# Bi-directional WKV and mixture-of-experts kernel on one core: one scan run over the other, shared outputs added in a second array, and a new order around layer 0's end

## The chip, the core and the metric

The kernel runs as one program on one core of a Trainium2 chip. Its time is the device time of one execution in microseconds (us); the figure for a kernel is the median of its timed runs, and lower is better. A core has the engines TensorE (PE), VectorE (DVE), ScalarE (ACT), GpSimd (POOL) and SyncE (SP), each with a queue of its own that runs in order, and 16 DMA engines that the queues feed.

## What is computed

x is [4, 512, 512]: 4 batches of 512 tokens of 512 channels, 2048 tokens in all. Two layers follow each other, x = x + ffn_l(cond_l(x, k)), with the same k (named fside) for both. The condition is a WKV in both directions of the sequence. For a batch and a channel:

```python
tf    = sigmoid(sum(time_emb))                       # one number of a batch
decay = exp(-exp(w)) * (0.5 + 0.5 * tf)
ek, ekv = exp(minimum(k, 30)), exp(minimum(k, 30)) * k
# forward:  a_t = a_{t-1} * decay + ekv_t,  b_t = b_{t-1} * decay + ek_t   -> nf, df
# backward: the same from the last token to the first                     -> nb, db
euk = exp(minimum(u + k, 30))
num = nf + nb - ekv + euk * k
den = df + db - ek + euk
out = sigmoid(x) * (num / maximum(den, 1e-8)) * (0.8 + 0.2 * tf)
```

Layer 0's ffn is an RMS norm, a router that sends each token to 2 of 8 experts (hidden width 256) and one shared expert of width 256 for all tokens. Layer 1's has 32 experts of hidden width 352, 6 for a token with a capacity of 512 tokens each, and a wider shared expert.

## The kernel before

Tokens are taken in 16 tiles of 128 (tile t belongs to batch t // 4). `acc` holds x in SBUF as rows of tokens, `kA` holds k turned to channels by tokens, `zT` the condition's output in the same form, both in 16 columns of 128 channels by 512 tokens. Two arrays in HBM, `xa` and `xb`, collect layer 0's output by rows; the routed experts add their rows to the one and the other in turn.

**Scan loop.** It runs over 16 units n (batch b = n // 4, channel chunk c = n % 4), one unit further in each stage: `turn(n + 3)` turns k's rows `kr` to `kA` (PE, then an ACT copy) and, after a batch's last chunk, issues the load of the next batch's `kr`, of which there is one buffer; `front` (L406, L408) and `front_exps` (L414) make ek and euk; `mid` multiplies by k (L425, L426) and calls `scans`, which runs four scans of 512 steps on DVE, forward (L263) and reversed (L264), for ek and for ekv. `sums` (L431) adds forward, reversed and own term on PE in PSUM, three products for den and three for num, and ACT makes r = 1 / den by Relu, Ln and Exp (L440 to L442). `back` (L449 to L452) corrects r once and multiplies num, r and the sigmoid of x into `zT`. The constants of w, u and tf are built ahead of the loop (L211 to L221).

**What else stands in the loop.** A batch later, its condition is turned back to rows (`row_turn`, `row_out`) and written to HBM (`z0d`), the router's logits follow, and routing in small DVE steps: `route_v` (the norm's scale, L501), `route_max`, `route_top` (r0sm, L291), `route_pos`, `route_pay`, `route_slots`, and POOL writes the slot tables by indirect DMA (L353). The shared expert runs for tiles 0 to 5 at units 7, 10 and 13 (`pairs0`): `share_up` (PE), `share_silu` (ACT), `share_hid` (DVE), `share_turn` and `share_down` (PE), `share_add` (L612, DVE, on top of `acc`, written to xa). `exps1_upto` makes layer 1's ek and euk on ACT (L627, L628) into columns that are free. Ahead of the loop, POOL zeroes the tables and all of xb in 16 writes (L254), and the last three tiles of x are copied to xa (L571).

**Tail.** After the loop come batch 3's rows (pz) and routing and the shared tiles 6 to 12.

**Routed layer 0.** `routed(0, ...)` goes through the slots of 128 tokens. Each gathers rows of z (POOL, L768), turns them (`turn_rows`, PE pza L781, scaling to zgT on ACT L785), multiplies by gate and up (L833, L837), forms the hidden rows on POOL (hrow, L844), turns them (phT, L795), multiplies by down (pout, L809) and adds rows to xa or xb (L814, POOL). Each turning is done one slot later, so a last `turn_hidden`, `copy_hidden` and `put_out` stand behind the loop over experts; branches on the experts' counts (L891) stand between. Beside it DVE works through `wkv1` (L907), layer 1's WKV: four scans, two adds of forward and reversed (L915, L916), a reciprocal (L921).

**Late tiles and second condition.** Behind the last turning the shared expert runs for tiles 13 to 15 (from `LATE`). Then the z1 stage (L960 to L985) goes through the 16 tiles: load xa and xb, add, turn (pt), sigmoid on ACT, product with `kA` on DVE (L975), logits (plg, L977), turn to rows (pz, L982), copy (zr) and write. The logits lg (L990) and layer 1's shared expert (L1058) follow.

**Order.** In the scan loop and the tail the orders of ACT, PE and DVE are those of the code; in routed layer 0 those of POOL, PE and ACT (`manual_schedule`). All other orders (SP throughout, POOL in the loop, DVE in routed layer 0, everything in the z1 stage) are chosen by the scheduler.

Of the kernel before, what the change touches and what calls it, by code (L numbers as in the profile page):

```python
# [25 lines left out]
DEN_MIN = 1e-8  # L26
EXP_LN = "natural_log_exp_and_others"
# [3 lines left out]
def adaln_ffn_kernel(  # L31
# [90 lines left out]
    def load_k(b):  # L122
        kr = wk.tile([P, TB, D], F32, tag="kr", name=f"kr{b}", bufs=1)
        nc.sync.dma_start(kr, kf[b * S : (b + 1) * S, :].rearrange("(i p) c -> p i c", p=P))
        return kr
# [54 lines left out]
    kr = wk.tile([P, TB, D], F32, tag="kr", name="kr0", bufs=1)  # L180
    for i in range(TB):
        nc.scalar.dma_start(kr[:, i, :], kf[i * P : (i + 1) * P, :])
    load_x(0)
    gaten = acc[:E1, NT - 3, :]
# [9 lines left out]
            engines={mybir.EngineType.Activation, mybir.EngineType.PE, mybir.EngineType.DVE}  # L194
# [20 lines left out]
    for l in range(2):  # L215
# [8 lines left out]
        decay.append(dec)  # L224
# [20 lines left out]
    for tb, width in ((table0, 3), (table1, 2)):  # L245
        blank = wk.tile([P, NCOL * width], F32, name=f"blank{width}", tag="lgT", bufs=1)
        bv = blank.rearrange("p (c w) -> p c w", w=width)
        nc.gpsimd.memset(bv, 0.0)
        nc.gpsimd.memset(bv[:, :, 0], EMPTY)
        nc.gpsimd.dma_start(tb.rearrange("(p c) w -> p (c w)", p=P), blank)  # L250
    zero = wk.tile([P, D], F32, name="zero", tag="zr", bufs=TB)
    nc.gpsimd.memset(zero, 0.0)
    for t in range(NT):
        nc.gpsimd.dma_start(xb[t * P : (t + 1) * P, :], zero)  # L254


    L = S - 1

    def scans(l, b, c, ek, ekv, df, dx, nf, nx):

        dec = decay[l][:, c, b : b + 1]
        for v, f, r in ((ek, df, dx), (ekv, nf, nx)):
            nc.vector.tensor_tensor_scan(f, dec.to_broadcast([P, S]), v, 0.0, ALU.mult, ALU.add)  # L263
            nc.vector.tensor_tensor_scan(  # L264
                r[:, L - 1 :: -1],
                v[:, L:0:-1],
                dec.to_broadcast([P, L]),
                0.0,
                ALU.add,
                ALU.mult,  # L270
            )

# [113 lines left out]
    def turn(n):  # L386

        nonlocal kr
# [4 lines left out]
        for i in range(TB):  # L393
            nc.tensor.transpose(pk[:, i * P : (i + 1) * P], kr[:, i, c * P : (c + 1) * P], ident)
        nc.scalar.copy(kA[:, c, b * S : (b + 1) * S], pk)
        if c == NC - 1 and b + 1 < NB:
            kr = load_k(b + 1)
            load_x(b + 1)

    def front(n):  # L400
# [4 lines left out]
        ek = wk.tile([P, S], F32, tag="ek", name=f"ek{n}", bufs=2)  # L405
# [706 lines left out]
```

## Time and profile before

| what | value |
|---|---|
| median of 3 runs | 1581.71 us (1581.02 to 1586.45) |
| the profiled execution | 1576.35 us, with a span of 1574.6 |
| mean granted clock of TensorE | 0.969 |
| PE busy | 1441.3 us (92%), weight loads beside it 858.7 |
| DVE busy | 681.8 us (43%) |
| POOL busy | 582.0 us (37%) |
| ACT busy | 407.1 us (26%) |
| DMA | 184.97 MB, 117 GB/s over the span |

All lines further on come from one profiled execution. Its own time is 1576.35 us; the span, from the first instruction to the last, is 1.75 shorter. Times in the text count from the span's start. In the rows of 40 slices a slice is 39.4 us, and a digit is the busy share in tenths; PEclk is the clock that TensorE was granted, in tenths of full speed. A row of the groups names line, engine, operation and tile, then the busy time, the mean of one instruction, and the idle time ahead of it with what ended it. PE was busy for 92% of the span, but at different clocks: in the stretch from 550 to 600 us it was granted 0.69 on average.

### The profile page before, as it was taken

What the parts mean: (1) busy time and instruction counts of PE and PEld (TensorE: products, weight loads), DVE (VectorE), ACT (ScalarE), POOL (GpSimd) and SP (SyncE); (2) the same over time, 40 slices, a digit from 0 to 9 for tenths busy, and PEclk for the clock granted to TensorE, in tenths of its full rate; (3) what the DMA queues carried; (4) which work ended last, traced back from release to release, by engine and by line L of the source; (5) the groups of instructions that cost most, each with busy time, mean ns of one, the idle gap of its engine ahead of it and who ended that gap; (6) DMA issues with size and microseconds to landing.
All of it is one profiled execution on the core that took longest, in us unless ns stands there. A gap on an engine that the chain in (4) does not pass through costs nothing. (4 is left out here: it accounts for less than half of the span.)

```text
span 1574.6 us, 16451 instructions
## 1 busy us (share of the span) xinstructions
PE 1441.3 (92%) x5097; PEld 858.7 (55%) x5097; DVE 681.8 (43%) x1192; ACT 407.1 (26%) x969; POOL 582.0 (37%) x576
## 2 busy tenths in 40 slices
PE   4978988989778698999999999999999999999997
PEld 2444555757556484444444565555655555555554
DVE  6897965999990045341111222222222222222221
ACT  4755634464344232000000111111111111111110
POOL 3010234666555100046662333344334344343332
PEclk8999989999999969999999999999999999999999
DMA  9201114454545652001115464666645495555442
GB/s 350 88 28 41 41 41 167 84 114 69 134 96 133 179 179 92 0 1 56 34 66 163 119 175 100 172 175 163 171 93 156 107 289 107 153 163 145 113 104 36
DMA packets 117179, 184.97 MB, mean 117 GB/s; under 512 B 19928, under 2 KB 65004, under 8 KB 117016
## 3 DMA queue, kind: packets, MB, share of 16 engines
q1 hardware_dynamic: 80120, 122.14, 22.8%
q0 software_dynamic: 36336, 60.04, 20.3%
q8 instruction: 66, 1.08, 0.3%
q10 hardware_dynamic: 576, 1.05, 0.2%
q14 instruction: 81, 0.66, 0.1%
HBM read 152.07 MB, written 52.64 MB: 130 GB/s over the span
## 5 line engine op out<-in xcount | busy, mean ns | idle before, releaser
L809 PE MATMUL pout<-w,hT 128*128 128x512 f32 (+1 forms) x432 | 202.8, 602 | 3.7 <-ACT hT L800 2.9
L833 PE MATMUL pgate<-w,zgT 128*128 128x352 f32 (+1 forms) x656 | 193.2, 438 | 10.9 <-PEq L891 6.7
L837 PE MATMUL pup<-w,zgT 128*128 128x352 f32 (+1 forms) x656 | 189.6, 432 | 0.0
L814 POOL DMA_INDIRECT out_dram<-ob,put x52 | 83.0, 1596 | 281.1 <-DVE ob L813 137.4
L768 POOL DMA_INDIRECT acc<-z1d,put x119 | 123.6, 1038 | 134.7 <-PE pza L781 59.9
L353 POOL DMA_INDIRECT table<-pay,r1sloti x96 | 93.6, 975 | 199.3 <-DVE hid L1061 172.4
L849 DVE SCALAR_TENSOR_TENSOR hrow<-pup,tab,sgt 128x352 f32<-128x352 f32 x84 | 49.1, 584 | 254.1 <-issue 131.2
L833 PEld LDWEIGHTS pgate<-w,zgT 128*128 128x128 f32 x656 | 122.8, 195 | 66.0 <-issue 17.5
L837 PEld LDWEIGHTS pup<-w,zgT 128*128 128x128 f32 x656 | 123.0, 191 | 49.0
L813 DVE COPY ob<-pout 128x512 f32<-128x512 f32 x84 | 58.1, 692 | 174.7 <-PE pout L809 167.3
L809 PEld LDWEIGHTS pout<-w,hT 128*128 128x128 f32 (+1 forms) x432 | 77.5, 194 | 71.3 <-issue 54.7
L353 POOL DMA_INDIRECT table<-r0pay,r0sloti x32 | 36.1, 1128 | 182.8 <-DVE r0sloti L343 137.8
L781 PEld LDWEIGHTS pza<-ident,acc 128*128 128x128 f32 x584 | 72.7, 142 | 53.8 <-issue 27.7
L781 PE MATMUL pza<-ident,acc 128*128 128x128 f32 x584 | 88.2, 276 | 12.9 <-DMA acc<-z0d,put 9.8
L804 ACT COPY hT<-phT 96x128 f32<-96x128 f32 x84 | 22.1, 263 | 287.4 <-DVE hT L802 282.8
L768 POOL DMA_INDIRECT acc<-z0d,put x51 | 69.7, 1367 | 71.9 <-PE pgate L833 27.2
L1058 PE MATMUL g<-zT,w 128*128 128x512 f32 (+1 forms) x192 | 88.6, 605 | 4.4 <-DVE lg L990 4.4
L791 ACT COPY zgT<-pza 128x256 f32<-128x256 f32 x103 | 38.4, 373 | 209.1 <-DVE zgT L790 153.4
L809 PE MATMUL pout<-zT,hT 128*128 128x512 f32 (+1 forms) x192 | 87.8, 592 | 0.0
L795 PE MATMUL phT<-ident,hrow 128*96 128x128 f32 (+1 forms) x322 | 55.9, 276 | 33.3 <-DVEq L891 15.0
L1058 PE MATMUL u<-zT,w 128*128 128x512 f32 (+1 forms) x192 | 86.3, 592 | 0.0
L1067 PE MATMUL o<-w,hid 128*128 128x512 f32 (+1 forms) x192 | 83.8, 592 | 0.0
(277 smaller groups left out, 2158.4 us busy)
## 6 DMA issues: line engine op xcount, KB each, us to landing
w<-in_L_ffn_w_dram SPq DMA_DIRECT2D x44, 704.0 KB
zT<-in_L_ffn_w_dram SPq DMA_DIRECT2D x20, 704.0 KB
w<-in_L_ffn_w_dram SPq DMA_DIRECT2D x22, 512.0 KB
zT<-in_L_ffn_w_dram SPq DMA_DIRECT2D x10, 512.0 KB
w<-in_L_ffn_w_dram SPq DMA_DIRECT2D x22, 192.0 KB
xb<-zero POOLq DMA_DIRECT2D x16, 256.0 KB
acc<-in_x_dram SPq DMA_DIRECT2D x4, 1024.0 KB
z0d<-zr SPq DMA_DIRECT2D x16, 256.0 KB
```

Of the source, the lines that this page charges most:

```text
L353: ins = nc.gpsimd.indirect_dma_start(out=table, out_offset=bass.IndirectOffsetOnAxis(ap=sloti[:, t, j : j + 1], axis=0), in_=pay[:, t, j, ...
L768: nc.gpsimd.indirect_dma_start(out=rows(e, s), out_offset=None, in_=zd, in_offset=bass.IndirectOffsetOnAxis(ap=put_at[:, e * NS + s : e * ...
L781: nc.tensor.transpose(pza[which][:, c * P : (c + 1) * P], rows(e, s)[:, c * P : (c + 1) * P], ident)
L795: nc.tensor.transpose(phT[:m, j * P : (j + 1) * P], hrow[:, f : f + m], ident)
L809: nc.tensor.matmul(po, hT[:m, j, :], dv[:m, j, :], start=(j == 0), stop=(j == nf - 1))
L813: nc.vector.tensor_copy(row, po)
L814: nc.gpsimd.indirect_dma_start(out=outs[n % len(outs)], out_offset=bass.IndirectOffsetOnAxis(ap=at, axis=0), in_=row, in_offset=None, boun ...
L833: nc.tensor.matmul(pg, zt[:, c, :], gv[:, c, :], start=(c == 0), stop=(c == NC - 1))
L837: nc.tensor.matmul(pu, zt[:, c, :], uv[:, c, :], start=(c == 0), stop=(c == NC - 1))
L849: nc.vector.scalar_tensor_tensor(hrow, pu, tab[:, col, 1:2], sgt, ALU.mult, ALU.mult)
L1058: nc.tensor.matmul(p[:m], wv[:, c, f : f + m], zT[:, c, cols], start=(c == 0), stop=(c == NC - 1))
L1067: nc.tensor.matmul(po, hid[:m, j, i * P : (i + 1) * P], dv[:m, j, :], start=(j == 0), stop=(j == len(FCH) - 1))
```

## The change

- **Scans.** The decay is held below 1 (`NEAR_1`). With om = 1 - decay^2, a reversed scan of v whose first column is then multiplied by 1 / om, followed by a forward scan of the result, gives (forward + reversed - own) / om. So the exponent of ek gets a bias of ln(om), and the sum comes out of one array. The scans work in place on `v`, which holds ek and ekv side by side; `sums` has two products for each output instead of three, and `wkv1` drops both adds.
- **k's rows.** `kr` has two buffers; batch 1's load is issued before the loop, and that of batch b + 2 at the end of batch b.
- **Shared outputs.** `share_put` takes the place of `share_add`: ACT copies the product to SBUF and SP writes it to xb's rows, instead of a DVE add to x. x itself is written to xa by SP, a batch at a time, and only xb's three late tiles are zeroed.
- **Routing.** The steps stand one to four units later: `route_v` at the next unit ahead of `front_exps`, `route_top` and `route_pay` at c = 3, `route_pos` and `route_slots` at the next batch's c = 0, with the slot writes spread over three units. The writes of all batches are now in the group that doesn't wait for each other. `share_hid` stands behind `back`. POOL's order is that of the code, too.
- **Routed layer 0.** DVE's order, `wkv1` included, is that of the code. The last turning is returned as `finish()`, and tile 13's share_up, share_silu and share_hid stand ahead of it. The late tiles' outputs go to columns of `zT`.
- **z1 stage.** SP's order is that of the code: xa and xb of the three late tiles first, then blocks of four tiles (1 MB), block 0's xb into a free column of zT, the others into buffers of their own. The order of the tiles' work is unchanged.

```diff
-        kr = wk.tile([P, TB, D], F32, tag="kr", name=f"kr{b}", bufs=1)
+        kr = wk.tile([P, TB, D], F32, tag="kr", name=f"kr{b}")
...
     load_x(0)
+    krs.append(load_k(1))
...
-        decay.append(dec)
+        nc.vector.tensor_scalar(dec, dec, NEAR_1, None, ALU.min)
+        om = const.tile([P, NC, B], F32, name=f"om{l}")
+        nc.vector.tensor_scalar(om, dec, -1.0, 1.0, ALU.mult, ALU.add)
+        nc.vector.scalar_tensor_tensor(om, dec, 1.0, om, ALU.add, ALU.mult)
+        lom = const.tile([P, NC, B], F32, name=f"lom{l}")
+        nc.scalar.activation(lom, om, AF.Ln)
+        inv = const.tile([P, NC, B], F32, name=f"inv{l}")
+        nc.vector.reciprocal(inv, om)
+        cap = const.tile([P, NC, B], F32, name=f"cap{l}")
+        nc.vector.tensor_scalar(cap, om, E30, None, ALU.mult)
+        decay.append((dec, cap, lom, inv))
...
+    def blank_tables():
...
-    for t in range(NT):
-        nc.gpsimd.dma_start(xb[t * P : (t + 1) * P, :], zero)
...
-    def scans(l, b, c, ek, ekv, df, dx, nf, nx):
-
-        dec = decay[l][:, c, b : b + 1]
-        for v, f, r in ((ek, df, dx), (ekv, nf, nx)):
-            nc.vector.tensor_tensor_scan(f, dec.to_broadcast([P, S]), v, 0.0, ALU.mult, ALU.add)
...
+    def scans(l, b, c, v):
+
+        dec, _, _, inv = (m[:, c, b : b + 1] for m in decay[l])
+        for h in range(2):
             nc.vector.tensor_tensor_scan(
...
+                v[:, h, ::-1], dec.to_broadcast([P, S]), v[:, h, ::-1], 0.0, ALU.mult, ALU.add
             )
+        nc.vector.tensor_scalar(v[:, :, 0], v[:, :, 0], inv, None, ALU.mult)
+        for h in range(2):
+            nc.vector.tensor_tensor_scan(v[:, h, :], dec.to_broadcast([P, S]), v[:, h, :], 0.0, ALU.mult, ALU.add)
...
-            kr = load_k(b + 1)
             load_x(b + 1)
+            if b + 2 < NB:
+                krs.append(load_k(b + 2))
...
+            nc.scalar.activation(v[:, 0, :], v[:, 0, :], AF.Exp, bias=decay[0][2][:, c, b : b + 1])
+            nc.scalar.activation(euk, euk, AF.Exp)
...
-            nc.tensor.matmul(p, m, f, start=True, stop=False)
-            nc.tensor.matmul(p[:, :L], m, r[:, :L], start=False, stop=False)
...
+            nc.tensor.matmul(p, m, d, start=True, stop=False)
             nc.tensor.matmul(p, m, o, start=False, stop=True)
...
-        zr = wk.tile([P, D], F32, tag="zr", name=f"zr{t}", bufs=TB)
+        zr = wk.tile([P, D], F32, tag="zr", name=f"zr{t}", bufs=3)
...
-    nc.sync.dma_start(xa[LATE * P :, :], xf[LATE * P :, :])
...
-    def share_add(t):
-        nc.vector.tensor_tensor(acc[:, t, :], shared_up.pop(t), acc[:, t, :], ALU.add)
-        nc.sync.dma_start(xa[t * P : (t + 1) * P, :], acc[:, t, :])
+    def share_put(t):
+
+        so = wk.tile([P, D], F32, tag="so", name=f"so_rows{t}")
+        nc.scalar.copy(so, shared_up.pop(t))
+        nc.sync.dma_start(xb[t * P : (t + 1) * P, :], so)
...
+        if n == 1:
+            for t in range(LATE, NT):
+                nc.gpsimd.dma_start(xb[t * P : (t + 1) * P, :], zero)
+        if n == 2:
+            blank_tables()
+        if c == 2 and b < NB:
+            nc.sync.dma_start(
+                xa[b * S : (b + 1) * S, :].rearrange("(i p) c -> p i c", p=P), acc[:, b * TB : (b + 1) * TB, :]
+            )
         front(n + 1)
+        if c == 2 and b >= 1:
+            route_v(b - 1)
         front_exps(n + 1)
-        if c == 3 and b >= 1:
-            route_pos(b - 1)
+        if c == 0 and b >= 2:
+            route_pos(b - 2)
...
+        for t in pairs0.get(n - 2, ()):
+            share_put(t)
...
-        for t in pairs0.get(n - 1, ()):
-            share_hid(t)
-        if c == 3 and b >= 1:
-            route_slots(b - 1)
+        if b >= 2 and c < 3:
+            if c == 0:
+                route_slots(b - 2)
+            write_slots(b - 2, 3 if c < 2 else 2)
         if c == 2 and b >= 1:
             route_max(b - 1)
+        if c == 3 and b >= 1:
+            route_top(b - 1)
+            route_pay(b - 1)
         if n == NU:
             share_up(early)
         if n:
             back(n - 1)
-        if c == 1 and b >= 1:
-            route_v(b - 1)
-        if c == 2 and b >= 1:
-            route_top(b - 1)
-            route_pay(b - 1)
-        for t in pairs0.get(n - 2, ()):
-            share_add(t)
+        for t in pairs0.get(n - 1, ()):
+            share_hid(t)
...
-        turn_hidden()
-        copy_hidden()
-        put_out(due, last[(E - 1) % 2], E, ob[3])
-        return ahead, pza, phT, pout
...
-    late_out = [acc[:, NT // 2 + h, :] for h in range(NT - LATE)]
...
+    late_out = [zT[:, h, :S] for h in range(NT - LATE)]
...
-            nc.vector.tensor_tensor(df[:, :L], df[:, :L], dx[:, :L], ALU.add)
-            nc.vector.tensor_tensor(nf[:, :L], nf[:, :L], nx[:, :L], ALU.add)
...
+            share_up(LATE, pza[0])
+            share_silu(LATE)
+            share_hid(LATE)
+            finish()
+            for t in range(LATE + 1, NT + 1):
+                if t < NT:
+                    share_up(t, pza[(t - LATE) % 2])
+                    share_silu(t)
+                    share_hid(t)
+                share_turn(t - 1, phT)
+                share_down(t - 1, po=pout[t % 2])
+                nc.scalar.copy(late_out[t - 1 - LATE], pout[t % 2])
...
-            nc.sync.dma_start(acc[:, t, :], xa[tok, :])
-            other = zp.tile([P, D], F32, tag="other", name=f"other{t}", bufs=8)
-            summand = nc.sync.dma_start(other, xb[tok, :]).ins
...
+    others = {t: zT[:, t - LATE, 2 * S : 3 * S] for t in late}
+    with tc.manual_schedule(engines={mybir.EngineType.SP}):
+        for t in late:
+            nc.sync.dma_start(acc[:, t, :], xa[t * P : (t + 1) * P, :])
+            nc.sync.dma_start(others[t], xb[t * P : (t + 1) * P, :])
+        for b in range(NB):
+            lo, hi = b * TB, min(b * TB + TB, LATE)
+            rows = slice(lo * P, hi * P)
+            many = zp.tile([P, hi - lo, D], F32, name=f"many{b}", bufs=1) if b else zT[:, :, S : 2 * S]
+            nc.sync.dma_start(acc[:, lo:hi, :], xa[rows, :].rearrange("(i p) c -> p i c", p=P))
+            summand = nc.sync.dma_start(many, xb[rows, :].rearrange("(i p) c -> p i c", p=P)).ins
```

## The prediction

> **What bounds the kernel now.** I read the page first: times by engine and the 40 slices.
>
> ```profile
> span 1574.6 us, 16451 instructions
> ...
> PE   4978988989778698999999999999999999999997
> ...
> DVE  6897965999990045341111222222222222222221
> ...
> PEclk8999989999999969999999999999999999999999
> ```
>
> TensorE is nearly full from slice 17 to the end (layer 1's shared and routed experts), and the diff touches nothing there. What can move lies in the first 15 slices of 39.4 us. Next the table by stage:
>
> ```profile
> 50.00:100.00 50.00, 40.96 (x150) 22.95 (x148) 46.34 (x101) 30.43 (x55) 0.00 (x0) 0.97 0.12 42
> 100.00:150.00 50.00, 42.85 (x156) 23.45 (x156) 41.91 (x91) 29.55 (x55) 10.16 (x8) 0.99 0.15 53
> 150.00:200.00 50.00, 45.79 (x145) 24.17 (x146) 46.54 (x105) 29.69 (x56) 9.93 (x8) 0.94 0.09 32
> 200.00:250.00 50.00, 45.20 (x170) 29.86 (x169) 24.69 (x85) 19.27 (x39) 17.43 (x19) 0.93 0.15 52
> ...
> 550.00:600.00 50.00, 43.13 (x256) 40.64 (x256) 22.03 (x35) 19.38 (x33) 0.00 (x0) 0.69 0.59 205
> ```
>
> Columns are PE, weight loads, DVE, ACT, POOL busy, then clock. Up to 212 us the scan loop is bound by DVE (46.3 of 50); DVE's own waits say where it loses time. From 212 to 260 PE carries the chain (shared tiles 6 to 12), from 262 to 523 too (routed layer 0). In 550 to 600 PE is "busy" at a clock of 0.69: that stage is a matter of waiting and of clock. Waits, then, for the two places (the second view is the timeline, the third the clock by single microseconds):
>
> ```profile
> PE pk L394 <- DMA kr<-in_fside_BxSxS_dram: 12.6, 3, 8.2
> DVE r0sm L291 <- ACT r0pr L288: 3.8, 1, 3.8
> ```
> ```profile
> 43.34 0.69 DVE L449 SCALAR_TENSOR_TENSOR t<-den,r 128x512 f32<-128x512 f32 x1 [6.87 <-ACT r L442]
> ...
> 535.45 0.85 SPq L964 DMA_DIRECT2D acc<-xa  x2
> ```
> ```profile
> 567.00:568.00 1.00, 1.00 (x6) 1.00 (x7) 0.00 (x0) 0.00 (x0) 0.00 (x0) 0.50 0.82 277
> ...
> 582.00:583.00 1.00, 1.00 (x7) 0.77 (x5) 0.68 (x1) 0.74 (x2) 0.00 (x0) 0.53 0.96 356
> 583.00:584.00 1.00, 1.00 (x11) 0.83 (x9) 0.77 (x3) 0.84 (x3) 0.00 (x0) 1.00 0.01 4
> ```
>
> PE stood 8.2 us for the second kr load (issued 22.55, landed 35.7), and DVE stood 6.87 us behind it.
>
> **Part 1, start and scan loop (DVE's path, 14.36 to 212.76 us).**
> - kr in two buffers, the second load issued at about 4 us instead of 22.55. Some 4 MB lie before its end; at the 350 to 400 GB/s of these microseconds that is 12 to 14 us, and PE asks at about 29. The 6.87 us go. Next late is the exponent chain, 0.55 us before L449 one unit earlier: kept.
> - New constants: per layer six small DVE steps (0.2 us each, as L211 to L221) and one Ln on ACT (0.21, as L219), ahead of the first kA copy on ACT's queue, because ACT waits twice for DVE: +2.1 us (0 to +2.5).
> - Scans: four of 1.20 us per unit before and after; the reversed form has the same 1.20 (L264). So the scan of a scan saves DVE nothing in layer 0; it saves PE two products per unit, 4 x 0.43 us. PE waits for DVE there, so I cost this at nothing; it only gives PE slack.
> - Between the scans a 128x2 scaling that must see the second scan end: its own 0.2, and 0.1 of overlap lost (1.12 pitch of 1.20): 0.3 x 16 = +4.8. In-place scans are not in the trace; in-place L450 and L452 cost 691 ns as the others do, so 0 extra, never less, and up to the rival below.
> - share_add leaves DVE: 6 in the loop at 0.64 pitch = -3.8. ACT gets copies of 0.59; ACT has 30 of 50 us.
> - Waits: route_v (1.77 and 1.60 us), route_top behind route_max (3.81), share_add (1.02) are cured by moving the steps to the next unit: -8.2; the wait for PE's product at 211 (1.44) goes too. I keep the wait of 1.67 for the logits, and allow 2.1 of new waiting where PE and ACT carry 15 us of row turning and shared products in one unit (units 9, 10, 13): those units' r is ready 10 to 13 us after the scans, against 10 to 11.5 us of DVE work.
>
> Sum: -6.9 + 2.1 + 4.8 - 3.8 - 8.2 - 1.4 + 2.1 = -11.3 (ends -15 and -5).
> - POOL: slot writes spread over three units and no longer wait for each other (2.4 us apart at 204 to 223, 1.28 in the group that didn't wait). Batch 3's eight writes take 10 us from slots that are ready 15 us after the loop; gathers could start 14 us before PE's tail ends. Hidden, with that slack. Zeroing falls from 16 to 3 tiles, and x goes to xa from SBUF in 4 writes of 1 MB: bytes early are the same, about 14 MB to 45 us. SP's queue holds the third kr load behind PE's turning, and writes behind it; nobody waits there.
>
> **Part 2, tail and first routed slots.** PE reached the row turning at 214.6, 1.84 after DVE's last product, because of its own backlog; with 1.7 us less per unit it is there: -1.5. The 45 us of PE work to 260.2 stay. Then gathers no longer wait for share_add (POOL stood 11.4 us; PE 1.22, 3.70, 1.07): -6.0. But ACT now copies the last two shared tiles before its last four exps: after PE's last product come 0.6 + 1.28 (table) + 2.5 + 1.28 = 5.7 us before the first zgT, where it was 2.0. That is +3.7, and about +1.5 for a clock fallen in that gap. Net -0.8, taken as 0 to stay at the nearest rows (-3 to +3). wkv1 gets 25 us lighter on DVE, but DVE ended 50 us before PE: nothing.
>
> **Part 3, late tiles and the second condition (523.94 to 602.33 us).** PE stood 5.49 us for POOL's branch before the last turning. Tile 13's product now fills it, from ACT's scaling end, 522.4. Cold clock, 5.5 us; last turning and product 2.7 (at 530.6); xa's last scatter lands 2 us later than before, loads at 537.3. The rest of the late tiles is the same PE work and ends near 547.5, as before, also because tile 15's share_hid now stands on DVE behind the sums of tiles 13 to 15, which wait for DMA until 543.5; PE's last turning waits for it, 1 to 2 us.
> Then the gain: before, 13 xa loads came first, xb loads only at 547.75 when the pool was free, first turning 552.5. Now three tiles and the first block are in, others land to 563 at 0.73 us per 256 KB. First logit product near 553 (before 557.5). From there at full clock: 16 x 0.98 (logits) + 28 x 0.61 (turnings) = 32.8; eight last row turnings stand behind three row buffers and their writes (2.6 us for three and a copy, 1.1 against 0.6): +4; last write and copy of lg 3.3: 593, less some overlap, 592. At half clock the same work takes 3.6 us per tile as measured: 606.
> [...] The trace shows the halving (0.50 from 553), and 30 us of it with PE busy 1.00; but at 583 it came back in a run of transposes. So I take the row: half clock from 553 until the run of five turnings (tile 0 to 4), some 12 us: 598, -4.5. Never dropping: 592, -10. The whole range is -10 to +4.
>
> **Sum.** The profiled execution took 1576.35 (span 1574.6 and 1.75 around it). -11.3 - 1.5 - 0 - 4.5 = -17.3: 1559.0. The median of the timed runs is 5.4 above the profile (1581.71): 1564.
>
> **Rivals.**
> - Clock never drops in the z1 stage (PE gaps at 548 to 553 hold 2.4 us of turnings in 5.4): 5.5 less, 1558.5. Chance 0.22. Against: at 224.7 to 227.7 a like mix dropped it.
> - Clock stays at half to 606: 1572.5. Chance 0.14.
> - Loop not freed: ACT and PE set units 9 to 14, the moved steps only move their waits, -4 in place of -11.3: 1571.5. For it: ACT waits for PE's products 11 us there. Against: DVE waited for r once only. Chance 0.09.
> - Slower: in-place scans. All 64 scans of layer 0 lie on DVE's path; a surcharge of 0.27 us each eats the 17.3, 0.4 us makes the kernel slower by over 0.5%; at half as much again (0.6 us x 64 = 38, less 17) it gives 1603. Chance 0.05; the in-place rows above speak against it.
> - My own, 0.50: 1564, own spread 6.
>
> A measurement tells about 0.5% (7.9 us) from no change. Faster by more: 0.50 x 0.94 + 0.22 + 0.14 x 0.6 + 0.09 x 0.65 = 0.83; same 0.12; slower 0.05. Range 1548 to 1576: from below the never-dropping clock, by the loop's better end, to past the half clock and the loop not freed.
>
> **What will show it.** No wait of PE for kr and none of 3.8 us at r0sm; the DVE loop ends near 201; the first routed product about 13 us earlier and its zgT 5.7 us after the last shared product; share_up before the last turning near 510 in new time; xb loads before the last late copy; clock 0.5 for 10 to 15 us in the z1 stage; layer 1's first product near 585. I am wrong if scans take over 1.3 us, if DVE waits for r in several units, or if the clock doesn't follow this.

## The result, and the profile after

| | before | changed |
|---|---|---|
| median | 1585.78 us (7 runs, 1578.81 to 1589.08) | 1574.94 us (7 runs, 1565.78 to 1575.59) |
| profiled execution, span | 1576.35, 1574.6 | 1565.78, 1563.8 |
| mean clock | 0.969 | 0.963 |

The ratio is 0.9927 (95% interval 0.9899 to 0.9956): faster by 0.7%. The spans of the two profiles differ by as much as the medians, 10.8 us; the forecast was 17.3. The changed kernel's seven executions fall in two groups, 1565.8 and 1567.5 us at a mean clock of 0.963 and 1574.0 to 1575.6 at 0.956 to 0.959, and its profile is the fastest of them, so spans of single profiles are compared with a doubt of some 10 us. First the page of the changed kernel, the rows that were shown of before:

```profile
span 1563.8 us, 16280 instructions
...
PE   5778888989788788999999999999999999999997
...
DVE  7999844999991145431111222222222222222221
...
PEclk9889889989998888999999999999999999999999
```

The granted clock is lower over the first 16 slices taken together, not higher (0.91 from 0 to 630 us, before 0.93). By stage (the same columns as before: PE, weight loads, DVE, ACT, POOL, then clock):

```profile
50.00:100.00 50.00, 38.28 (x137) 20.80 (x136) 48.03 (x100) 30.04 (x55) 0.00 (x0) 0.90 0.11 42
100.00:150.00 50.00, 40.06 (x149) 22.34 (x150) 47.82 (x106) 31.98 (x59) 9.15 (x8) 0.97 0.09 32
150.00:200.00 50.00, 37.96 (x108) 18.95 (x107) 41.07 (x95) 28.42 (x52) 9.39 (x8) 0.86 0.12 43
200.00:250.00 50.00, 47.31 (x190) 33.16 (x189) 15.38 (x70) 21.50 (x44) 20.51 (x22) 0.93 0.21 68
550.00:600.00 50.00, 41.99 (x256) 35.26 (x255) 21.41 (x48) 20.69 (x34) 0.00 (x0) 0.78 0.54 191
```

To 150 us DVE is full (48 of 50). From 150 to 200 no engine is: DVE falls to 41, PE to 38 at a clock of 0.86. DVE's waits in the loop (line, releaser, total, times, longest) name two that were not there:

```profile
DVE v L519 <- ACT rsg L512: 4.7, 1, 4.7
DVE r0posi L336 <- PE pos L548: 3.8, 1, 3.8
```

DVE's timeline in an early unit shows the new scans (start, duration; the pair of a line merged):

```profile
24.22 2.33 DVE L278 TENSOR_TENSOR_SCAN v<-dec,v 128x512 f32<-128x512 f32 x2
26.59 0.23 DVE L281 TENSOR_SCALAR v<-v,inv 128x2 f32<-128x2 f32 x1
26.85 2.34 DVE L283 TENSOR_TENSOR_SCAN v<-dec,v 128x512 f32<-128x512 f32 x2
29.11 0.67 DVE L457 SCALAR_TENSOR_TENSOR t<-den,r 128x512 f32<-128x512 f32 x1
```

In place, reversed or forward, a scan still takes 1.2 us. From the first scan to L457 it is 4.89 us. Before's four scans took 4.48, from the first of these rows to the second:

```profile
198.06 1.22 DVE L263 TENSOR_TENSOR_SCAN df<-dec,ek 128x512 f32<-128x512 f32 x1
...
202.54 0.17 DVE L324 CAST r0posi<-pos 128x32 int32<-128x32 f32 x1
```

That is 0.41 more in each unit. The loop's first multiplication by k (`mid`) starts 1.85 us later than before; the first row is before's, the second the changed kernel's:

```profile
14.36 0.69 DVE L425 TENSOR_TENSOR ekv<-ek,kA 128x512 f32<-128x512 f32 x1
```
```profile
16.21 0.69 DVE L435 TENSOR_TENSOR v<-v,kA 128x512 f32<-128x512 f32 x1
```

The z1 stage of the changed kernel, in single microseconds:

```profile
548.00:549.00 1.00, 0.66 (x3) 0.66 (x4) 1.00 (x3) 0.78 (x2) 0.00 (x0) 0.58 1.03 381
...
560.00:561.00 1.00, 1.00 (x7) 1.00 (x6) 0.00 (x0) 0.00 (x0) 0.00 (x0) 0.50 0.92 192
561.00:562.00 1.00, 1.00 (x7) 0.77 (x6) 0.20 (x1) 0.60 (x1) 0.00 (x0) 0.59 1.00 325
562.00:563.00 1.00, 0.82 (x7) 0.59 (x7) 0.86 (x2) 0.99 (x2) 0.00 (x0) 1.00 0.71 263
```

Half clock lasts 13 us here, 30 before. (In the traces of e1, e5, e6 and e8 below, whose z1 code is the same, the longest of the 64 turnings pt took 422 to 477 ns and the shortest 272; here it is 477 and 272. The median is 421 in e1 and e6, 273 in e5, e8 and here.) Set against each other, the milestones of the two traces say where the 10.8 us came from (each line is the change in the distance from the milestone above):

| milestone | before | changed | change |
|---|---|---|---|
| DVE's loop ends | 212.76 | 207.18 | -5.6 |
| last shared product of the tail ends | 260.2 | 252.5 | -2.1 |
| first hidden turning (phT) of routed layer 0 | 276.2 | 268.2 | -0.3 |
| last up product of routed layer 0 starts | 515.9 | 512.1 | **+4.2** |
| layer 1's first product | 602.33 | 592.56 | -6.0 |
| end of the span | 1574.6 | 1563.8 | -1.0 |

### The profile page after: what moved, and what is told of

The parts are those of the page before. It is cut to its first block, busy times and chain, and to the rows that moved or that the text cites. A ratio compares the mean times of both kernels' runs of the same rounds, so it can differ in the third digit from the quotient of the medians.

```text
span 1563.8 us, 16280 instructions
## 1 busy us (share of the span) xinstructions
PE 1424.2 (91%) x5033; PEld 849.2 (54%) x5033; DVE 678.2 (43%) x1189; ACT 415.2 (27%) x984; POOL 564.6 (36%) x563
## 5 line engine op out<-in xcount | busy, mean ns | idle before, releaser
L862 PE MATMUL pgate<-w,zgT 128*128 128x352 f32 (+1 forms) x656 | 198.3, 448 | 19.9 <-ACTq L920 9.3
L862 PEld LDWEIGHTS pgate<-w,zgT 128*128 128x128 f32 x656 | 126.1, 200 | 76.1 <-issue 17.5
L810 PEld LDWEIGHTS pza<-ident,acc 128*128 128x128 f32 x584 | 71.8, 141 | 44.9 <-issue 27.5
L797 POOL DMA_INDIRECT acc<-z0d,put x51 | 62.5, 1225 | 58.5 <-issue 17.0
L862 PE MATMUL pgate<-zT,zgT 128*128 128x352 f32 x256 | 81.0, 459 | 0.0
## 6 DMA issues: line engine op xcount, KB each, us to landing
w<-in_L_ffn_w_dram SPq DMA_DIRECT2D x22, 512.0 KB, 8.5
zT<-in_L_ffn_w_dram SPq DMA_DIRECT2D x10, 512.0 KB, 4.5
xa<-acc SPq DMA_DIRECT2D x4, 1024.0 KB, 11.2
```

The lines of the kernel that those rows point to most:

```text
L797: nc.gpsimd.indirect_dma_start(out=rows(e, s), out_offset=None, in_=zd, in_offset=bass.IndirectOffsetOnAxis(ap=put_at[:, e * NS + s : e * ...
L810: nc.tensor.transpose(pza[which][:, c * P : (c + 1) * P], rows(e, s)[:, c * P : (c + 1) * P], ident)
L862: nc.tensor.matmul(pg, zt[:, c, :], gv[:, c, :], start=(c == 0), stop=(c == NC - 1))
```

## The experiments

How far a milestone can be trusted: seven profiles of the same loop code (the changed kernel, e3, e4, e6, e8, e9, e12) have its last product start between 202.7 and 206.5. Distances under about 2 us are not read as effects from single traces. The z1 stage scatters more: from the last late product to layer 1's first it took 47.6 to 52.2 us in six traces with the same code from tile 13 on (the changed kernel 48.2, e1, e3, e5, e6, e7), and 55.3 in before's. "Changed" is the changed kernel's trace.

| run | ratio to before (95%) | span | loop's last product | first phT | last up product | layer 1's first product |
|---|---|---|---|---|---|---|
| before | 1 | 1574.6 | 212.1 | 276.2 | 515.9 | 602.3 |
| changed | 0.9927 (0.9899, 0.9956) | 1563.8 | 206.5 | 268.2 | 512.1 | 592.6 |
| e1_kr_single | 0.9945 (0.9929, 0.9961) | 1570.9 | 205.3 | 266.8 | 514.0 | 599.2 |
| e2_scan_only | 1.0358 (1.0290, 1.0426) | 1640.7 | 206.6 | 268.8 | 514.1 | 669.0 |
| e11_scan_and_order | 0.9953 (0.9932, 0.9974) | 1576.5 | 210.5 | 274.3 | 517.7 | 603.7 |
| e5_loop_both | 0.9870 (0.9804, 0.9935) | 1559.0 | 196.0 | 263.1 | 507.6 | 587.4 |
| e3_exps_first | 0.9942 (0.9920, 0.9965) | 1565.8 | 206.1 | 267.6 | 510.6 | 595.0 |
| e6_so_kept | 0.9882 (0.9825, 0.9940) | 1569.4 | 205.0 | 262.8 | 510.0 | 594.7 |
| e7_code_shift | 0.9869 (0.9804, 0.9934) | 1564.1 | 206.5 | 268.3 | 508.8 | 592.7 |
| e8_finish_first | 0.9865 (0.9807, 0.9924) | 1560.6 | 202.8 | 264.4 | 511.3 | 587.2 |
| e4_z1_old_loads | 0.9914 (0.9885, 0.9942) | 1566.7 | 204.1 | 264.5 | 512.0 | 594.1 |
| e9_z1_tail | 0.9919 (0.9890, 0.9949) | 1565.7 | 206.0 | 267.5 | 511.0 | 587.8 |
| e12_fill | 0.9942 (0.9912, 0.9972) | 1561.3 | 202.7 | 264.2 | 508.4 | 588.9 |
| e10_three | 0.9860 (0.9819, 0.9900) | 1554.9 | 198.5 | 262.2 | 506.6 | 583.1 |

The intervals of all variants but e2 overlap that of the changed kernel; what they tell is mostly read in their traces. The runs of e5 to e8 were set against one group of runs of before, and all four came to 0.9865 to 0.9882: these ratios do not tell the four edits apart.

### The loop

**e1, one buffer for k again.**

```diff
-        kr = wk.tile([P, TB, D], F32, tag="kr", name=f"kr{b}")
+        kr = wk.tile([P, TB, D], F32, tag="kr", name=f"kr{b}", bufs=1)
...
-    krs.append(load_k(1))
...
+            krs.append(load_k(b + 1))
             load_x(b + 1)
-            if b + 2 < NB:
-                krs.append(load_k(b + 2))
```

> The changed kernel with one buffer for kr again, each load issued behind the last turning of the batch before. Own theory: DVE's path has no slack early in the loop, so the 6.87 us wait comes back (near 43 us) and carries to the loop's end, from 207.2 to about 214, and to the kernel: +6 to +7 us against the changed kernel. Rival, late units set by PE and ACT: DVE waits 9.5 us in units 13 to 16 of the changed kernel, and a later DVE fills part of that; loop end +2 to +4, kernel +2 to +4.

The wait of 6.87 us did not come back, and the loop ended within 1.2 us of the changed kernel's. The load was issued at 17.24 us (before: 22.55) and PE turned batch 1's rows at 26.83 without a wait (before: 35.76). Before, the copy of x to xa stood ahead of it on SP's queue for 2.7 us, and 4 MB of zeros were going to xb; the copy and most of the zeros are gone from these microseconds in the changed kernel. The other edits thus cure this wait without the second buffer, and with them in place the buffer adds nothing measurable; the buffer alone was not run. Neither theory had that. The span of e1 is 7.1 us longer than the changed kernel's, near the first theory's number, but not for its reason: the time is lost behind the loop, in code that is the same.

**e2, the scan of a scan alone,** and **e11, the same with DVE's order by hand.** e2 is the kernel of before with the new constants, `scans`, `front`, `mid`, `sums` and `wkv1`. e11 adds:

```diff
+            engines={
+                mybir.EngineType.Activation, mybir.EngineType.PE, mybir.EngineType.DVE, mybir.EngineType.Pool
+            }
+        ):
+            for n in range(10):
+                wkv1(n)
```

> The kernel of before with the scan of a scan alone (both layers), all else as before. Own theory: the scans save DVE nothing in layer 0; the changed kernel's own trace shows 4.89 us for the group of four scans and the scaling where before it was 4.48, so 16 x 0.41 = +6.6 us on DVE's path, less 1.4 for PE's product at the loop's end: loop end 212.8 to about 218, and DVE's lighter work in routed layer 0 takes a part of the 11.2 us back that PE waited for hidden rows on POOL there. Kernel +1 to +6 us against before. Rival, the scans are the gain: PE's two products fewer for each unit and DVE's 25 us less in layer 1's WKV make it faster by 5 us or more.

> The kernel of before with the scan of a scan, and with DVE's order in routed layer 0 by hand (layer 1's WKV of the first ten units ahead of the slots, the rest at expert 1); all else as before. In e2 the scheduler had put the last six units behind the slots, where PE stood 78 us for them. Theory now: the loop ends near 206.6 as in e2, since PE's products set the late units and not DVE's scans; with the order by hand that gain carries, kernel -4 to -7 us against before, more than half of the whole change's 10.8. Rival, the prediction's sum: scan and constants cost DVE 5.5 us, kernel 0 to +5 against before.

e2 as a whole is 57 us slower for a reason outside the question: with DVE's order left to the scheduler, the last six units of layer 1's WKV came behind the slots. DVE did nothing from 400 to 500 us, and the z1 stage's first turning waited 78 us for it. The edit that gives routed layer 0's DVE order by hand is therefore needed for the scans. The loop's waits in e2 can be read all the same:

```profile
DVE t L451 <- ACT r L444: 2.5, 1, 2.5
DVE r0sm L297 <- ACT r0pr L294: 1.7, 1, 1.7
```

With the old routing places, the old single buffer and share_add on DVE, all waits of DVE from the loop's first `mid` to its last product came to 6.2 us (e11: 9.8), against 18.9 before. The wait behind k fell from 6.87 to 2.5 and 4.3, that for the router's exponents from 3.8 to 1.7, those for the logits and the square sums went or shrank. Two causes meet here. PE has 1.7 us less in each unit (two products, 4 x 0.43 us as recorded) and so is earlier where DVE meets it; and DVE itself comes later, as it starts 1.9 to 2.0 us later and does 5.3 to 5.6 us more. DVE's lateness alone would not end the loop earlier than before. So the 5.4 us by which it ended earlier in e2 (1.5 in e11, which the scatter covers) are the least that PE's lighter work gave there; how the rest divides is not shown. e11's timed runs are 0.5% below before (0.9953), about two thirds of the whole change's 0.7%. Its one profile has the loop's end at 210.5, not at the expected 206.6, and a span above before's, so the size rests on the timed runs, and no trace shows where it lies. The rest of the change (routing, shared outputs, the other orders) was not run alone.

**e5, two steps moved again.**

```diff
-    pairs0 = {7: (0, 1), 10: (2, 3), 13: (4, 5)}
+    pairs0 = {7: (0, 1), 10: (2, 3), 14: (4, 5)}
...
-        if b >= 2 and c < 3:
+        if 2 <= b < NB and c < 3:
...
             back(n - 1)
+        if n == NU:
+            route_slots(b - 2)
+            write_slots(b - 2, 3)
```

> The changed kernel with two moves in the loop: the third pair of shared tiles at unit 14 instead of 13 (where batch 2's rows are turned), and batch 2's slot numbers behind the last unit's products instead of ahead of them. Theory now: in units 13 to 16 PE's order sets the pace, and the moved routing steps stand where PE is late: the waits of 4.71 us (for the norm's scale) and 3.84 (for the positions) go, the loop's last product starts near 200 instead of 206.5, and PE loses no clock in gaps of 3.4 and 5.4 us; kernel -4 to -6 us. Rival, PE's work is only moved: what leaves unit 13 comes back in unit 14 or at the start of the tail, the last shared product ends within 1.5 us of 252.5, kernel within 1.5 us.

DVE's timeline from 140 us to the loop's end, the two longest waits in it:

```profile
165.39 0.69 DVE L459 TENSOR_TENSOR t<-num,t 128x512 f32<-128x512 f32 x1 [0.46 <-PE pz L477]
...
195.27 0.69 DVE L459 TENSOR_TENSOR t<-num,t 128x512 f32<-128x512 f32 x1 [0.87 <-PE num L446]
```

The waits of 4.7 and 3.8 us are gone and the last product starts at 196.0, 10.5 us earlier. The part of PE's work that moved to unit 16 takes half of it back: the last shared product starts at 246.6, 5.3 earlier, and the span is 4.8 shorter. Theory held, but for the clock: in the changed kernel it is 0.50 from 183 to 186 and from 197 to 203 us, at the end of gaps of 3.42 and 5.42 us, yet the mean is the same in e5 as there (0.91 from 140 to 180, 0.83 from 180 to 200).

### The start of routed layer 0

**e3** moves the last exponents ahead of the last two copies; **e6** does that and keeps the last two outputs out of the loop's pool:

```diff
+    exps1_upto(10)
     for t in (LATE - 2, LATE - 1):
         share_down(t, "den")
         share_put(t)
-    exps1_upto(10)
...
-        so = wk.tile([P, D], F32, tag="so", name=f"so_rows{t}")
+        so = so_late[t % 2] if t >= LATE - 2 else wk.tile([P, D], F32, tag="so", name=f"so_rows{t}")
...
+    so_late = [acc[:, NT - 3 + h, :] for h in range(2)]
```

> The changed kernel with the last four exponents of layer 1 moved ahead of the last two copies of shared outputs in ACT's order. Own theory: ACT's 5.7 us between the last shared product and the first scaling shrink to about 2, PE's first gate product starts near 254.9 instead of 258.8 and at full clock, so the first slot's products end near 258.5 instead of 265.3; kernel -5 to -6.5 us. Rival, given back later: POOL's gathers or the branches of routed layer 0 set the pace and take it back, kernel within 1.5 us.

> The changed kernel with the exponents ahead of the last copies, as in e3, and besides the last two shared outputs copied into rows of x's array that are free, so that no buffer of the loop's pool has a write to HBM outstanding when routed layer 0 begins. Theory now, from e3: the first scaling waits for the pool of the loop, which the last write holds (it lands near 258), not for ACT. With both gone the first gate product starts near 255 instead of 258.8, and at a higher clock; first hidden turning near 263 instead of 268; kernel -4 to -5 if it carries. Rival, the branches' waits give it back: first gate product earlier by 3 us or more, the last up product of routed layer 0 within 1.5 us of 512, kernel within 1.5 us.

ACT in e3, just ahead of the first slot:

```profile
254.13 1.28 ACT L764 ACT_TABLE_LOAD   x1
258.14 1.14 ACT L814 ACTIVATE zgT<-pza,chan 128x128 f32<-128x128 f32 x4 [2.73 <-DMA xb<-so_rows]
```

The first gate product stayed at 258.7 us, where 254.9 was expected. ACT is ready at 255.4 and now waits 2.73 us for the write of the last shared output: its tile lies in the loop's pool, and the tiles of routed layer 0 take that pool's place. The exponents had only hidden this. With e6 the first gate product starts at 254.7 (4.5 us behind the start of the last shared product, where it was 6.9 in the changed kernel) and the first hidden turning follows 12.6 behind it, where it was 16.3. Of these 3.7 us, 3.3 went again before the last up product, as the rival had it. The timeline of PE at the third branch of e6:

```profile
400.33 1.88 PE L839 MATMUL pout<-third,hT 128*128 128x512 f32 x4
409.86 1.65 PE L863 MATMUL pgate<-w,zgT 128*128 128x256 f32 x3 [7.65 <-issue]
```

PE stood 7.65 us. The branch's own record (number, then nanoseconds and time) in that stretch:

```profile
L921 PEldq COMPARE_BRANCH  x1: 5587/5587/5587, 399.7 to 399.7; - x1
```

PE's branch was issued at 399.7 and took 5.59 us. The queue that the profile calls "instruction" (q8) carried a packet of 16 KB that ended at 403.8, 1.5 us ahead of the branch's end, and another that began between 407 and 409 and took about 1.0 us, before PE went on at 409.86. At this branch of the changed kernel, too, the branch's end and PE's next product come 1.4 and 1.2 us behind the ends of two packets (407.32 and 410.90). And all 14 of PE's branches of over 2.5 us in routed layer 0 of the traces of before and of the changed kernel end 1.3 to 1.5 us behind the end of such a packet. So the author's reading is that PE waited for one packet at the branch and for another right behind it; what the packets held, and that PE waited for them, is not shown. In the trace of before the branch took 3.82 us, most of it behind products that were queued, and the second packet began after PE had gone on: PE stood 1.17 us.

**e7, PE's code shifted,** to see whether the branch waits change with it.

```diff
+    pk = bank("tr", "pad")
+    for i in range(64):
+        nc.tensor.transpose(pk[:, i % 4 * P : (i % 4 + 1) * P], ident, ident)
     for n in range(3):
```

> The changed kernel with 64 turnings of the identity, which nobody reads, at PE's start: 128 more instructions for PE, in time in which it waits for k. Theory: PE's long waits at the branches of routed layer 0 (19.8 us before seven gate products, 13.2 in the kernel of before) [...] the sum of these waits changes by 3 us or more in one direction or the other, with nothing else moved but the start by at most 3 us. Rival, the branch waits for another engine: the sum stays within 2 us of 19.8.

The sum of the branch waits ahead of gate products was 18.2 us against 19.8: by the stated measure the rival, though at the third branch 4.31 fell to 2.69. The stretch from the first hidden turning to the last up product was 240.5 us (changed 243.9; all other variants 243.0 to 247.5; before 239.7), since the gate products behind two branches now took 1.99 us for eight instead of 3.42 and 3.47, and behind two more 2.3 and 2.5 instead of 3.57 and 3.60. At three of these four branches the wait was nearly the same in both traces (2.6 to 3.0 us), so the slower products there do not follow from longer waits. That the code's place decides how long the stretch is, is not shown.

**e8, the last turning ahead of tile 13 again.**

```diff
+            finish()
             share_up(LATE, pza[0])
             share_silu(LATE)
             share_hid(LATE)
-            finish()
```

> The changed kernel with tile 13's shared product behind the last turning again, as in the kernel of before. By the prediction tile 13 fills the wait of 5.49 us: +4 to +5.5 us here. Theory now: PE itself cannot go on behind the last branch (the product waited 4.00 us there), so the wait only moves to the last turning, and what is lost is the cover of ACT's copies: late tiles end 0 to 1.5 us later, kernel 0 to +1.5.

PE in e8, then PE in the changed kernel, behind the last branch:

```profile
519.30 0.69 PE L824 MATMUL phT<-ident,hrow 128*128 128x128 f32 x2 [5.50 <-POOLq L920]
520.50 3.41 PE L838 MATMUL pout<-w,hT 128*128 128x512 f32 x4 [0.52 <-ACT hT L829]
523.75 7.07 PE L594 MATMUL pza<-third,zT 128*128 128x256 f32 x32
```
```profile
512.75 1.88 PE L838 MATMUL pout<-w,hT 128*128 128x512 f32 x4
518.64 6.49 PE L594 MATMUL pza<-third,zT 128*128 128x256 f32 x16 [4.00 <-ACTq L920]
```

From the last up product to the last late product it is 30.9 us in e8 and 32.2 in the changed kernel; the expectation had e8 the same or later. Tile 13 fills little: PE waits 4.00 us in front of it, too, and its 16 products then run at a granted clock of 0.50 from 518 to 524 us (6.49 us against 3.6 for the next tile's, at 1.00). What it waits for is on ACT in the changed kernel:

```profile
515.25 3.29 ACT L257 ACTIVATE third<-third,chan 128x256 f32<-128x256 f32 x8
```

ACT scales `third`, the shared expert's weights, which tile 13's product reads. It ends at 518.5, and the product starts at 518.64, though PE's own branch was through at 514.8. To fill the gap, this scaling would have to come earlier; that was not tried. PE's order alone can win only what lies between ACT's end (517.8 in e8) and the last turning (519.3).

### The z1 stage

**e4, the old loads,** **e9, more row buffers and lg in a tile of its own,** **e12, PE kept busy.**

```diff
+        nc.sync.dma_start(acc[:, t, :], xa[tok, :])
+        other = zp.tile([P, D], F32, tag="other", name=f"other{t}", bufs=8)
+        summand = nc.sync.dma_start(other, xb[tok, :]).ins
```
```diff
-        zr = zp.tile([P, D], F32, tag="zr", name=f"zr1_{t}", bufs=3)
+        zr = zp.tile([P, D], F32, tag="zr", name=f"zr1_{t}", bufs=8)
...
-    lg1 = rt.tile([P, NT, E1], F32, name="lg1")
+    lg1 = nfac.rearrange("p b q -> p (b q)").rearrange("p (t e) -> p t e", e=E1)
```
```diff
+            for _ in range(6):
+                nc.tensor.matmul(pza[1], ident, nfac.rearrange("p b q -> p (b q)"), start=True, stop=True)
```

> The changed kernel with the z1 stage's loads as before: tile by tile, xb in eight buffers of the z1 pool, SP's order left to the scheduler. Own theory: the first turning waits 4 to 5 us behind the last late tile again and the clock stays at half for longer; layer 1's first product comes 4 to 10 us later than the changed kernel's 592.6, kernel +4 to +10. Rival, hidden: the stage ends on the rows' writes and lg in any case, within 1.5 us.

> The changed kernel with eight row buffers in the z1 stage instead of three, and layer 1's logits copied into a constant tile that is no longer used, so that the copy waits for no pool. Theory: the last turnings wait 3.2 us for row buffers, and lg stands from 580.5 (last logits) to 591.8 behind the rows' writes because its tile lies where the stage's pools lay; layer 1's first product then starts 0.7 us behind the last row copy: 592.6 less 3.2 less 2.7, kernel -4 to -6 us. Rival: layer 1's shared expert, its weights or its pools need the same writes, within 1.5 us.

> The changed kernel with six products of the identity by a constant (128x512, read by nobody) behind the last late tile's product, where PE waits 0.7 and 1.7 us for the first sums and sigmoids of the z1 stage. Theory: the clock falls in that gap, at about 548, and is at half until 562; kept busy, PE goes on at full clock, the stage's first 14 us of work take 7 to 9, and layer 1's first product comes 3 to 6 us earlier; kernel -3 to -6 us. Rival: the clock falls all the same in the next wait, or the stage ends on transfers, kernel 0 to +2 (the fill delays the first turning by 1 us).

e4: the first turning waits 6.54 us for its sum and starts at 549.7 instead of 545.6, and the lower clock lasts some 20 us (0.78 from 545 to 550, 0.50 to 565, 0.67 to 570). Yet layer 1's first product came only 1.5 us later than in the changed kernel, and the time is no worse: the rival. From the last late product the stage took 51.5 us, inside the scatter of 47.6 to 52.2, so what the new order of loads is worth cannot be read here. Before's stage took 55.3; where the rest of the difference comes from, no run shows.

e12: the clock, in stretches of 5 us:

```profile
545.00:550.00 5.00, 4.85 (x17) 2.20 (x16) 2.48 (x5) 0.23 (x1) 0.00 (x0) 1.00 0.95 324
550.00:555.00 5.00, 3.35 (x31) 3.22 (x31) 3.67 (x7) 3.92 (x6) 0.00 (x0) 1.00 1.04 394
555.00:560.00 5.00, 4.75 (x44) 4.40 (x42) 1.91 (x4) 2.38 (x5) 0.00 (x0) 1.00 0.63 196
560.00:565.00 5.00, 5.00 (x49) 5.00 (x49) 4.07 (x8) 2.83 (x6) 0.00 (x0) 1.00 0.38 136
```

Where the changed kernel had 0.50 (549 to 561 us), the clock is 1.00, through turnings and 32-column products alone. In the ten other traces of the changed kernel and its variants the longest turning pt took 422 to 478 ns, in e12 329. So this kind of work did not halve the clock by itself here, and the gap is the likelier cause. That rests on one trace. The stage became only 1.7 us shorter (46.5 us from the last late product to layer 1's first, where it was 48.2), which the scatter covers, and the expected 3 to 6 us do not show in the time (0.9942): the fill itself ran 5.65 us, partly at a low clock (0.66 from 540 to 545), and held the first turning back; at the end the clock fell again (0.80 and 0.52 from 575 to 585), and PE waited 4.32 us for lg.

e9: layer 1's first product came at 587.8 instead of 592.6, as expected (the stage took 43.4 us, below all others), and nothing of it reached the end. DVE, then PE, in layer 1's first microseconds:

```profile
592.41 0.69 DVE L296 TENSOR_REDUCE r1mx<-nfac 128x16 f32<-128x512 f32 x1 [5.04 <-DMA w<-in_L_ffn_sw_dram]
```
```profile
614.76 10.56 PE L1116 MATMUL o<-w,hid 96*128 96x512 f32 x20 [2.69 <-DVE hid L1110]
```

The router's first reduction waits 5.04 us and starts at 592.4; that its tile still lies in that pool's place is the likely reason, not tried. The routing then stands ahead of `hid` on DVE, PE waits 2.69 us for it, and both kernels have their first routed gate product of layer 1 at 845.4 and 845.5.

**e10, the edits of e5, e6 and e8 together.**

> The changed kernel with the edits of e5, e6 and e8 together. If they add up as their own traces had them up to the z1 stage (last shared product -5.3, first hidden turning a further -3.7 behind it, late tiles -1.3): layer 1's first product near 583 instead of 592.6, kernel -6 to -10 us against the changed kernel, ratio to the kernel of before about 0.986 to 0.989. Rival, given back: as in e6 and e9 an earlier start of routed layer 0 is spent at its branches; only e5's part stays, -4 to -5, ratio about 0.990.

The median was 1555.73 us against 1578.47 for before on the same chip, the ratio 0.986 (0.982 to 0.990). The span is 8.9 us below the changed kernel's and layer 1's first product comes at 583.1, both as expected, but the parts do not add up on the way. The last shared product starts only 0.6 us earlier than in the changed kernel (251.3 against 251.9; e5: 246.6), and the last late product 6.2 us earlier (538.1 against 544.3), of the 10.3 expected by there. Another 3.2 us come in the z1 stage (45.0 us), whose code is unchanged; e8, with the same order ahead of it, had 44.9. It has the shortest span and the lowest ratio, and its interval ends where the changed kernel's (0.9899 to 0.9956) begins; from e5 to e8 it is not told apart.

## Why the prediction was right in sign, and its gain too large

The time, 1574.9, lies inside the range of 1548 to 1576, by one microsecond; the forecast of 1564 counted on 17.3 us and 10.8 came. (Before itself took 1585.8 beside the changed kernel, 4.1 more than in the runs that the forecast started from.) Two terms make up the shortfall, and smaller ones offset a part of it: the waits in the loop fell by 9.4 us instead of 14.4, and routed layer 0, taken as unchanged, became 4.2 us longer. By its own steps:

- **What bounds the loop.** The prediction took DVE as its bound up to 212 us, from 46.3 of 50 us. That holds from 50 to 100; its own next row, 100 to 150, has DVE at 41.9 and PE at 42.9. There both engines' work counts.
- **Second kr buffer, -6.9.** The wait went, but not for the reason given: e1 shows that it goes without the buffer, too. The sum counted it on top of everything else; the scan of a scan alone had already taken 2.6 to 4.4 us of it (e11, e2).
- **PE's two products fewer, "at nothing".** This is wrong. It was costed at nothing because PE waits for DVE in most of the loop. But DVE's waits in before's loop were nearly all for PE, or for ACT behind PE (6.87 us of them with the late load of k at the root). e2 and e11 have 6.2 and 9.8 us of waits instead of 18.9, and end the loop 5.4 and 1.5 us earlier though DVE has more to do; by the prediction's sum they would end it later. It is not what made the forecast too large: priced, it would have made it larger still, unless taken off the waits that it cures.
- **Moved routing steps, -8.2, and new waits, +2.1.** The new waits are the term that was mis-sized: 4.7 and 3.8 us, where 2.1 was allowed. The moved steps met PE and ACT in units 13 to 16. DVE's waits fell from 18.9 to 9.5, where the sum had -14.4 for all of them together. This is the rival "the moved steps only move their waits", in part: it was given 0.09, and the loop's -5.6 is nearer to its -4 than to -11.3. e5 shows that it was the places that cost, and not the move as such.
- **Scaling between the scans, +4.8.** 0.41 x 16 = +6.6. DVE's time in the loop outside its waits rose by 2.0 (179.5 to 181.5), where the sum had 1.0 with share_add's -3.8.
- **New constants, +2.1.** The loop's first `mid` began 1.85 us later: right.
- **Tail, -1.5:** -2.1.
- **First slots, 0:** -0.3. The net was right, with the right gap of about 6 us ahead of the first gate product, but a wrong cause beside the right one: e3 shows that the write of the last shared output holds the pool about as long as ACT's exponents did.
- **Routed layer 0 beyond its first slots, taken as unchanged: +4.2.** All traces with this code have this stretch longer than before's 239.7, by 0.8 us (e7) to 7.8. Between the two traces PE's waits at branches rose by 6.0 us and the slow gate products behind them by 6.0 (five branches with 3.4 to 3.75 us for eight products, mostly at a granted clock of 0.50, before one with 3.65; 1.96 at 1.00), one wait for hT by 1.1; waits for hidden rows on POOL fell by 6.9 and for gathers by 2.5. That is +3.7 of the 4.2. Whether the lighter WKV on DVE has a part in the hidden rows, where the prediction said "nothing", is not shown: a PE that stands longer at branches may wait less for POOL for that alone, and e7, with fewer slow products, waited 8.6 us for hidden rows (changed 4.3, before 11.2). Why the branches cost more is not settled. It shows with the scans alone: e2 and e11, without the other edits, have 19.6 and 18.6 us of waits there, before 13.9, the changed kernel 19.8.
- **Late tiles and z1, -4.5:** -6.0, the sum of +1.1 in the late tiles and -7.1 in the z1 stage. The six traces with the same code from tile 13 on lie between -1.2 and -6.6 against before, so how near the term came is in part luck. The clock did as the row had it: 0.50 for 13 us where "some 12" were written (e1 and e6, with the same code, had more slow turnings, medians of 421 ns against 273), back in a run of turnings, 1.00 through turnings in e12. Tile 13's product began where ACT's scaling ended, as written, and so filled little; the early loads could not be shown to be worth anything (e4).
- **In-place scans slow:** no; 1.2 us each.

## What to carry to other kernels

When one engine works for nine tenths of a loop, its few waits are where the gain is, and each names the engine whose work to cut: price a cut of that engine's work by those waits and not at nothing. Before two edits are added up, ask whether each alone cures the same wait. A step that is moved away from one wait can meet another: look at what the other engines do in the unit that it moves to. Before work is moved into a gap, look when its operands are ready; tile 13's weights were scaled by ACT in that very gap (3.29 us). A wait behind a branch need not be for another engine's work: look at the branch's own record, as in e6, where PE's took 5.59 us. And a tile with a write outstanding can hold up what takes its pool's place (2.73 us in e3).

## What the runs showed that was not expected

- At its third branch in e6 PE stood 7.65 us, in which two packets of 16 KB came on the instruction queue; at the same branch in the kernel of before it stood 1.17.
- A gap at a branch can be paid twice. In the traces of before, the changed kernel, e6 and e7, all six gaps of 3.75 us and more were followed by eight gate products that took 3.4 to 3.8 us instead of 1.97; gaps of 2.5 to 3.0 us went both ways. Behind the changed kernel's five gaps of 2.6 us and more, and before's of 3.93, the granted clock was 0.50 within half a us of PE's going on; behind before's of 2.51 and 2.79 it stayed at 1.00.
- Turnings and 32-column products alone kept the full clock (1.00) from 550 to 575 us, once a fill had carried PE over the gap (e12).
